# The last two QKV groups of the last head pair move one row block up in the program

## Chip, core and metric

The kernel runs on one core of a Trainium2 chip. The metric is the device time of one execution in microseconds (us). The program is written with a tile framework: a scheduler orders the instructions of every engine when the program is built, and pools hand out buffers. Each engine then runs its own list strictly in order, and so does the queue in which SyncE (SP) issues DMAs.

## What is computed

One transformer block over 2048 rows of 1024 columns, in float32: layer norm, causal attention with 16 heads of 64 columns and rotary embedding, output projection, layer norm and residual, and then a feed-forward part whose weights are stored as 4-bit codes with scales. Cut to the part that the change touches:

```python
q = (layernorm(x) @ Wq).reshape(b, s, 16, 64)        # k, v likewise
q, k = rotary(q), rotary(k)
logits = where(causal, q @ k.T, -1e9) / sqrt(64)
out = softmax(logits) @ v                            # per head
x = x + layernorm(out.reshape(b, s, 1024) @ Wo)      # then the feed-forward part
```

## The kernel before

Heads are worked on in eight pairs, m = 0 to 7. The 2048 rows are cut into four blocks of 512, J or c = 0 to 3.

**QKV groups.** `qkv(m, c, ...)` computes q, k and v of the pair m for the row block c. Each of the three is a sum of 24 matmuls with 512 columns (`mm3`, L112 to L114, each product in three parts), so a group has 72. The sum for q or k is copied out by ScalarE (ACT, L251), rotated on VectorE (DVE, L253 and L254) and GpSimd (POOL, L255 and L256), split into a high and a low part (ACT L120, DVE L121) and written to DRAM by L259, to `qs` or `ks`. v is copied (L241), transposed (PE, L244), split and written to `vs` by L249. The group first loads four tiles of the normalized input (`xc<-xd`, L222) and the rotation table (`tab`, L232).

**Attention.** `attend(h, J, ...)` handles one head and one block of 512 query rows. `scores` does two matmuls for each block of keys (L278, L280), a row maximum on DVE (L284 or L286), the exponential on ACT (L288), small DVE steps that combine the maxima and sums (L297 to L305, with one ACT step, L300), and the scaling of the probabilities on POOL (L310). `weighted` transposes the probabilities (PE, L320), splits them (ACT L120, DVE L121) and multiplies by v (L324, L325). The result of a head goes out by ACT L327 and DVE L328 and is written to `at` by L329. Keys, values and queries are loaded from DRAM by L335, L336 and L342.

**The last pair.** The loop over pairs 0 to 6 computes the groups of later pairs beside the attention. The groups (7, 2) and (7, 3) are left out of it and stand in the last loop, over J, for the pair m = 7. Before that loop the weight tile of the last part of the output projection is prepared (`last_wo`); after it come the other seven (`prep_wo`: load `wof` by L427, ACT L429, POOL L430), and then the projection of the first four row tiles (`attended`: load `af` by L456; `project`: L469 to L471), written to lie beside the last attention. All of these draw on the same four buffers of the tag `f4`: the table, the split results of q, k and v, the `wof` tiles and the `af` tiles.

**What sets the order.** The scheduler takes instructions by a priority that follows program order, as soon as its own model finds their inputs ready. A piece of the program that stands earlier is served first; one that stands later fills gaps. So the place of `group` in the loop does not fix when it runs, only who goes first where both could.

Of the kernel before, what the change touches and what calls it, by code (L numbers as in the profile page):

```python
# [57 lines left out]
def block_kernel(ctx, tc, x, wq, wk, wv, wo, gu_codes, gu_scales, d_codes, d_scales, cos_sin, out):  # L58
# [159 lines left out]
    def load_x(c):  # L218
        tiles = []
        for kp in range(4):  # L220
            tiles.append(slot("xc", [P, 2, 2, 512], FR, "xc"))
            load(f32(tiles[kp]), xd[c][:, kp])  # L222
        return tiles

    def prep_qkv(m, tags=("w", "w", "w")):
        behind = (None, high[-1], high[-1]) if m == 0 else (None,) * 3
        return [prep_w(w, m, sc, tag, b) for w, sc, tag, b in zip((wq, wk, wv), (0.125, 1.0, 1.0), tags, behind)]

    def qkv(m, c, ws, xs, ramp=False, pace=None):
        cs = slice(c * 512, (c + 1) * 512)  # L230
        tab = slot("f4", [P, 2, 512], F32, "tab")
        (A.dma_start if ramp else load)(tab, cos_sin[:, :, cs])  # L232
        for n, w in enumerate(ws):
            o = bank("S" if ramp and n != 1 else "F", "qkv")
            for k in range(KE):
                mm = mm3(o, w[k], xs[k // 2][:, :, k % 2, :], k == 0, k == KE - 1)
                if k == 0 and pace:
                    pace(mm, n)
            t1 = slot("t2", [P, 512], F32, "t1")
            if n == 2:  # L240
                A.copy(t1, o)  # L241
                pv = bank("F", "pv").rearrange("p (t n) -> p t n", t=4)
                for t in range(4):
                    T.transpose(pv[:, t, :], t1[:, t * P : (t + 1) * P], ident)  # L244
                vo = slot("f4", [P, 4, 2, 2, D], FR, "vo")
                src = pv.rearrange("p t (a d) -> p t a d", a=2)
                for a in range(2):
                    split(vo[:, :, a, 0, :], vo[:, :, a, 1, :], src[:, :, a, :])
                load(vs[m][cs].rearrange("(t p) a n -> p t (a n)", p=P), f32(vo.rearrange("p t a l d -> p t (a l d)")))  # L249
            else:  # L250
                A.copy(t1, o)  # L251
                sh = slot("t2", [P, 512], F32, "sh")
                V.stream_shuffle(sh, t1, [i ^ 1 for i in range(32)])  # L253
                V.tensor_tensor(t1, t1, tab[:, 0, :], ALU.mult)  # L254
                G.tensor_tensor(sh, sh, tab[:, 1, :], ALU.mult)  # L255
                G.tensor_tensor(t1, t1, sh, ALU.add)  # L256
                hl = slot("f4", [P, 2, 512], FR, "hl")
                split(hl[:, 0, :], hl[:, 1, :], t1)
                load((qs, ks)[n][m][:, :, cs], f32(hl))  # L259
# [71 lines left out]
    def load_kv(h, k, v, cs):  # L331

        m, r = h // 2, h % 2 * D
        for a in range(2):
            load(f32(k[a * D : (a + 1) * D, cs]), ks[m][r : r + D, a, cs])  # L335
        load(f32(v[:, cs.start // P : cs.stop // P]), vs[m][cs, h % 2, :].rearrange("(t p) n -> p t n", p=P))  # L336

    def load_q(h, q, J):

        m, r = h // 2, h % 2 * D  # L340
        for a in range(2):
            load(f32(q[a * D : (a + 1) * D]), qs[m][r : r + D, :, J * 512 : J * 512 + 512])  # L342
# [24 lines left out]
    def new_kv():  # L367
        return slot("hd", [P, S], FR, "k"), slot("hd", [P, NT, P], FR, "v")

    def new_q():  # L370

        q = slot("hd", [P, 2, 2, 512], FR, "q")
        return [q[:, 0], q[:, 1]]

    def attend(h, J, q, k, v, anchors):
        weighted(h, J, scores(J, q, k, anchors), v)
# [7 lines left out]
    def group(m, c, xs=None, pace=None):  # L384
        if m not in ws:
            ws[m] = prep_qkv(m)
        qkv(m, c, ws[m], xs or load_x(c), pace=pace)
# [47 lines left out]
    m = KE - 1  # L435
    kv = {}
    for J in range(NC):
        for h in (2 * m, 2 * m + 1):
            if J == 0:
                kv[h] = new_kv()  # L440
            load_kv(h, *kv[h], parts[J])
            if h % 2 == 0:
                qj = new_q()
            load_q(h, qj[h % 2], J)
        for h in (2 * m, 2 * m + 1):
            attend(h, J, qj[h % 2], *kv[h], anchors)
        if J in (1, 2):
            group(m, J + 1)


    wot = [prep_wo(k, "w" if k < 3 else "xc") for k in range(KE - 1)] + [last_wo]
# [388 lines left out]
```

## Time and profile before

| | |
|---|---|
| runs shown | 3012.16, 3017.91 and 3018.1 us, median 3017.91 us |
| profiled execution | 3014.01 us, of which the span of the trace is 3012.1 us |
| PE busy | 2917.0 us, 97% of the span, 14168 matmuls |
| DVE, ACT, POOL busy | 2035.8, 1698.4 and 953.0 us |
| mean granted TensorE clock | 0.991 |
| first and last matmul start of qkv with `xc` | 201.0 and 1339.4 us |

Times in the trace are counted from the start of the span. PE is the matmul engine, "SPq" the queue of SyncE. An entry such as "[2.77 <-DMA wof<-in_wo]" behind an instruction says that its engine sat idle for 2.77 us before it, and what ended this. A busy PE is not PE at its peak, since ends of matmuls are modelled and the clock may be lowered.

### The profile page before, as it was taken

The page shows a single profiled execution, that of the slowest core. Times are in us where ns is not written, and L with a number is a line of the kernel's source. Part 1 is how long each engine was busy: PE and PEld are TensorE (multiplying, and loading weights), DVE is VectorE, ACT ScalarE, POOL GpSimd, SP SyncE. Part 2 cuts the span into 40 slices and gives each one's busy share as a digit, 9 for nine tenths or more (in the row PEclk, how much of TensorE's full clock was granted, in tenths as well). Part 3 has the DMA queues.
Part 4 walks back from the last instruction along what each step waited for, and adds up shares of the span by engine and source line. Part 5 has one row for each costly group of instructions (what it writes and reads, how often), then busy time and mean ns, then how long its engine had stood idle before and what let it go on. Part 6 is the DMA issues. An engine that isn't in the chain of part 4 may idle for free.

```text
span 3012.1 us, 42532 instructions
## 1 busy us (share of the span) xinstructions
PE 2917.0 (97%) x14168; PEld 2409.7 (80%) x14168; DVE 2035.8 (68%) x4171; ACT 1698.4 (56%) x3569; POOL 953.0 (32%) x1055
## 2 busy tenths in 40 slices
PE   7989999999998999999999999999999999999998
PEld 6868888787887787777788788888888887888887
DVE  6567778886777778777665767776666677444347
ACT  4256667776666667667555655655555566333234
POOL 4344344443434343445322121222211223100034
PEclk9999999999999999999999999999999999999999
DMA  8787665757556468463456444444334444744446
GB/s 287 277 249 233 214 222 177 222 161 220 172 195 182 146 202 260 137 210 105 123 187 213 130 134 143 151 133 140 131 119 140 138 153 146 254 141 148 150 144 234
DMA packets 271740, 536.01 MB, mean 178 GB/s; under 512 B 22944, under 2 KB 113056, under 8 KB 255648
## 3 DMA queue, kind: packets, MB, share of 16 engines
q1 hardware_dynamic: 269344, 529.10, 54.6%
q10 hardware_dynamic: 2176, 4.19, 0.4%
q8 instruction: 112, 1.84, 0.3%
q14 instruction: 108, 0.88, 0.1%
HBM read 371.98 MB, written 161.22 MB: 177 GB/s over the span
## 4 chain that ended last, share of the span: by engine, by line
PE 79%; DMA 10%; DVE 4%; ACT 2%; POOL 2%; issue 1%; SPq 1%; POOLq 0%; ACTq 0%; DVEq 0%
PE bk L112 14%; PE bk L114 14%; PE bk L113 14%; PE pt L320 6%; PE qkv L112 4%; PE qkv L113 4%; PE qkv L114 4%; PE o L325 3%; PE o L324 3%; PE s L278 3%; PE s L280 3%; DMA wf<-in_wq 3%; PE pj L469 2%; PE pj L471 2%; PE pj L470 2%
## 5 line engine op out<-in xcount | busy, mean ns | idle before, releaser
L310 POOL TENSOR_SCALAR prob<-prob,rc 128x512 f32<-128x512 f32 (+3 forms) x640 | 405.4, 659 | 436.4 <-DVE rc L305 219.6
L112 PE MATMUL bk<-x,wt 128*128 128x512 f32 x1376 | 534.0, 390 | 2.7 <-ACT wt L120 1.8
L113 PE MATMUL bk<-x,wt 128*128 128x512 f32 x1376 | 535.2, 389 | 0.0
L114 PE MATMUL bk<-x,wt 128*128 128x512 f32 x1376 | 535.1, 389 | 0.0
L288 ACT ACTIVATE prob<-s,mxs 128x512 f32<-128x512 f32 (+3 forms) x640 | 402.6, 632 | 147.8 <-DVE mxs L286 90.6
L121 DVE TENSOR_TENSOR pw<-pt,pw 128x512 fp32r<-128x512 f32 (+3 forms) x640 | 378.4, 602 | 119.7 <-ACT pw L120 118.0
L534 ACT ACTIVATE ln<-cs,bias 128x512 f32<-128x512 f32 x520 | 360.0, 716 | 109.2 <-DVE m L541 25.4
L120 ACT CAST pw<-pt 128x512 fp32r<-128x512 f32 (+3 forms) x640 | 324.1, 527 | 171.6 <-PE pt L320 140.6
L320 PE MATMUL pt<-ident,prob 128*128 128x128 f32 x2176 | 345.5, 275 | 6.8 <-DVE pw L121 5.5
L320 PEld LDWEIGHTS pt<-ident,prob 128*128 128x128 f32 x2176 | 267.6, 141 | 61.7 <-issue 7.2
L112 PEld LDWEIGHTS bk<-x,wt 128*128 128x128 f32 x1376 | 258.2, 188 | 57.5 <-ACT wt L120 2.6
L286 DVE TENSOR_REDUCE mxs<-s 128x1 f32<-128x512 f32 x384 | 260.9, 681 | 60.0 <-PE s L280 59.1
L114 PEld LDWEIGHTS bk<-x,wt 128*128 128x128 f32 x1376 | 258.3, 188 | 53.8
L113 PEld LDWEIGHTS bk<-x,wt 128*128 128x128 f32 x1376 | 258.3, 188 | 53.5
L278 PE MATMUL s<-k,q 128*128 128x512 f32 (+3 forms) x640 | 265.7, 416 | 25.1 <-ACT prob L288 22.4
L325 PE MATMUL o<-pw,v 128*128 128x512 f32 (+3 forms) x640 | 247.3, 388 | 9.5 <-DVE pw L121 9.0
L324 PE MATMUL o<-pw,v 128*128 128x512 f32 (+3 forms) x640 | 244.3, 382 | 9.8 <-ACT pw L120 7.9
L112 PE MATMUL qkv<-xc,w 128*128 128x512 f32 x576 | 231.8, 402 | 10.3 <-ACT w L186 6.3
L113 PE MATMUL bk<-bt,at 128*128 128x512 f32 x616 | 239.6, 389 | 0.0
L114 PE MATMUL bk<-bt,at 128*128 128x512 f32 x616 | 238.8, 389 | 0.0
L112 PE MATMUL bk<-bt,at 128*128 128x512 f32 x616 | 238.7, 389 | 0.0
L280 PE MATMUL s<-k,q 128*128 128x512 f32 (+3 forms) x640 | 236.6, 372 | 0.0
(150 smaller groups left out, 5513.8 us busy)
## 6 DMA issues: line engine op xcount, KB each, us to landing
xc<-xd SPq DMA_DIRECT2D x96, 1024.0 KB, 9.3
q<-qs SPq DMA_DIRECT2D x128, 256.0 KB, 7.2
ast<-S SPq DMA_DIRECT2D x44, 512.0 KB, 3.9
cs<-in_gu_scales SPq DMA_DIRECT2D x172, 128.0 KB, 3.2
cs<-in_gu_codes SPq DMA_DIRECT2D x86, 256.0 KB, 3.0
A<-in SPq DMA_DIRECT2D x66, 256.0 KB, 2.0
S<-in SPq DMA_DIRECT2D x66, 256.0 KB, 3.2
ast<-A SPq DMA_DIRECT2D x33, 512.0 KB, 4.5
```

What stands on the lines that cost most here:

```text
L112: r = T.matmul(o, lhsT=w[:, 0], rhs=xx[:, 0], start=first, stop=False)
L113: T.matmul(o, lhsT=w[:, 0], rhs=xx[:, 1], start=False, stop=False)
L114: T.matmul(o, lhsT=w[:, 1], rhs=xx[:, 0], start=False, stop=last)
L121: return V.tensor_tensor(lo, src, f32(hi), ALU.subtract)
L278: mm = T.matmul(s, lhsT=q[:, 0, j * P : (j + 1) * P], rhs=k[:, b:e], start=True, stop=False)
L280: T.matmul(s, lhsT=q[:, 1, j * P : (j + 1) * P], rhs=k[:, b:e], start=False, stop=True)
L288: A.activation(prob[i][:, j, : e - b], s, AF.Exp, bias=mx, scale=sign, accum_out=sums[:, j % BATCH, i : i + 1])
L310: G.tensor_scalar(p, p, rc[:, jj % BATCH, i : i + 1], 0.0, ALU.mult, ALU.add)
L320: T.transpose(pt[:, j * P : (j + 1) * P], prob[kb // 4][:, j, kb % 4 * P : (kb % 4 + 1) * P], ident)
L324: T.matmul(o[:, cs], lhsT=v[:, kb, :], rhs=pw[:, 0, cs], start=kb == 0, stop=False)
L325: T.matmul(o[:, cs], lhsT=v[:, kb, :], rhs=pw[:, 1, cs], start=False, stop=kb == nk - 1)
L534: A.activation(ln, c8, AF.Prelu, bias=bias_of[ab], scale=ab[0], alpha=ab[2])
```

## The change

The group for block J + 1 was called after the attention on block J, for J = 1 and 2. Now the group for block J + 2 is called after the attention on block J, for J = 0 and 1. So the two groups (7, 2) and (7, 3) keep their work, buffers and inputs, and each stands ahead of one more call pair of `attend` than before: (7, 2) ahead of the attention on J = 1, and (7, 3) ahead of that on J = 2.

```diff
         for h in (2 * m, 2 * m + 1):
             attend(h, J, qj[h % 2], *kv[h], anchors)
-        if J in (1, 2):
-            group(m, J + 1)
+        if J in (0, 1):
+            group(m, J + 2)
```

## The prediction

> **What bounds the kernel now.** I read the page first, then the busy time in three stretches around the last head pair, then PE's waits, then the order of time there.
>
> ```profile
> PE 2917.0 (97%) x14168; PEld 2409.7 (80%) x14168; DVE 2035.8 (68%) x4171; ACT 1698.4 (56%) x3569; POOL 953.0 (32%) x1055
> ```
>
> PE is the bound nearly everywhere, so the change can only move time where PE idles or is slowed. The instruction orders of the two kernels as built show where that can be. On PE both lists hold 14170 instructions, the first 6370 and the last 6658 alike; on DVE, ACT, POOL and SP there is likewise a common head and a common tail. Laid on the trace, the differing PE rows run from 1271.7 us to about 1503 us. Everything outside is untouched, and inside no instruction is added or removed. The busy time (PE, PEld, DVE, ACT, POOL, then clock, DMA share and GB/s) in that region:
>
> ```profile
> 1264.00:1343.00 79.00, 77.25 (x426) 65.29 (x427) 57.65 (x161) 51.95 (x138) 38.50 (x49) 1.00 0.70 224
> 1343.00:1373.50 30.50, 22.26 (x118) 17.21 (x116) 25.85 (x54) 25.97 (x61) 23.51 (x21) 0.89 0.62 205
> 1373.50:1503.00 129.50, 124.27 (x635) 101.28 (x633) 83.67 (x201) 77.27 (x175) 50.27 (x63) 1.00 0.34 106
> ```
>
> PE idles 1.75 us in the first stretch, where the groups (7, 2) and (7, 3) fill it; 8.2 us in the second, between the last group and the first projection; 5.2 us in the third, spread over many waits under 1 us. The middle one matters. Its PE waits (total, times, longest):
>
> ```profile
> PE pt L320 <- DVE pw L121: 4.7, 2, 2.5
> PE o L324 <- ACT pw L120: 2.2, 1, 2.2
> PE s L278 <- ACT prob L288: 0.7, 1, 0.7
> PE o L325 <- DVE pw L121: 0.6, 1, 0.6
> ```
>
> And how the first two came about, in order of time, SP's queue first, then the engines:
>
> ```profile
> 1338.28 0.56 SPq L259 DMA_DIRECT2D ks<-hl  x1
> 1343.80 2.37 SPq L335 DMA_DIRECT2D k<-ks  x4
> 1346.21 1.53 SPq L427 DMA_DIRECT2D wof<-in_wo  x3
> 1348.51 0.55 SPq L249 DMA_DIRECT2D vs<-vo  x1
> 1355.53 0.93 SPq L336 DMA_DIRECT2D v<-vs  x2
> 1356.50 0.98 SPq L427 DMA_DIRECT2D wof<-in_wo  x2
> ```
> ```profile
> 1350.46 1.04 ACT L429 CAST wo<-wof 128x1024 fp32r<-128x1024 f32 x1 [2.77 <-DMA wof<-in_wo]
> 1351.72 0.33 PE L324 MATMUL o<-pw,v 128*128 128x128 f32 x1 [2.22 <-ACT pw L120]
> 1351.91 2.05 DVE L299 TENSOR_TENSOR cf<-mxs,nm 128x4 f32<-128x4 f32 x1
> 1355.31 1.09 PE L320 MATMUL pt<-ident,prob 128*128 128x128 f32 x4 [2.15 <-DVE pw L121]
> 1370.51 0.63 PE L320 MATMUL pt<-ident,prob 128*128 128x128 f32 x4 [2.52 <-DVE pw L121]
> ```
>
> Group (7, 3) writes its keys at 1338.28. SP reaches the load of the same keys and stands until the write has landed, at 1343.80; the first weight tile of the output projection is queued behind the four key loads and is issued at 1346.21. ACT reaches that tile's cast at 1347.69 and waits 2.77 us, the `pw` copy behind it is late, and PE loses 2.22 us. Then a DVE step of four elements takes 2.05 us (the median of L299 is 0.163 us) while POOL runs L430, and PE loses 2.15 us; a like pile-up on DVE costs 2.52 us at 1370.5. Also the clock drops:
>
> ```profile
> 1354.00:1358.00 4.00, 2.69 (x11) 2.43 (x12) 3.92 (x11) 3.95 (x10) 3.74 (x2) 0.50 0.68 221
> ```
>
> From the mean clock of the 4 us windows around it, half clock lasted from about 1352.7 to 1359.5 us. Four transposes took 1.09 us instead of 0.60. From 1355.31 to 1359.58 PE did work that takes about 2.15 us at full clock, so the slow clock cost about 2.1 us.
>
> **The change part by part.** Nothing is added. I weigh what is moved by the PE work in front of it: 0.227 us for a matmul of 512 columns (starts at 1338.08 and 1338.31), 0.113 us for a transpose, in each kernel's order.
>
> *The groups themselves.* Each still starts when the scheduler finds its input tiles. With PE work counted from one common row, k of (7, 2) ends after 25.5 us of work instead of 26.3, q and k of (7, 3) after 53.2 and 65.1 instead of 55.9 and 66.9; v of both ends at the same row in both kernels. So "one block sooner" is 1 to 3 us on the chip, not the length of a block. The matmuls are the same 144: 0 us. The cover is the attention beside them; PE's 1.75 us of idle in this stretch is the floor of what can be gained, and I take 0 here, between -1 and +1.5 us.
>
> *Who could use q, k and v sooner.* The key loads of J = 2 were issued by 1317 us and those of J = 3 by 1346 us; the first exponentials on them come at 1354 and 1407 us. So the attention on J = 2 and 3 was not waiting for the groups: gain 0.
>
> *Loads in SP's queue.* For (7, 2) the key write passes the value loads of the pair, one write of `at` and four query loads; its loads no longer stand ahead of a blocked queue. It also puts a key load ahead of `tab` of (7, 3), which was issued at 1305.74 and used at 1321.63: a delay of a few us is covered. The second half of the input tiles of (7, 3) is then free of the key write ahead of it; PE waited 0.09 us for it. Together 0.
>
> *The stall at 1350.* The keys of (7, 3) are ready 1.9 us of PE work sooner, and their split stands six DVE rows and four ACT rows further up. Their write passes four query loads and a write of `at`. So SP's stand ends about 1.9 to 2.5 us sooner, at about 1341.6; four key loads (2.4 us) and one query load that now lies between (0.6 us) follow, and the first `wof` is issued at about 1344.6 instead of 1346.2. With the 4.2 us of its transfer, ACT's wait shrinks from 2.77 to about 1.1 us: -1.6 us. The two scale loads moved behind `wof` feed a later stage and cost 0.
>
> *What is late next.* POOL's L430 and the fourth `wof`, which is issued when the first L430 ends (1353.94 and 1353.97), follow that shift. The fifth and sixth do not: they stand in SP's queue behind the value loads, which wait for `vs` to land. In the new DVE order one row maximum more (0.6 us) comes ahead of the last split of v, so `vs` is written 0 to 1.7 us later, and ACT reaches the fifth cast sooner. It had no wait before (1362.04); now 0 to 2.5 us. I take 0.8, so the gain left of this chain is 0.8 us.
>
> *The stall at 1370.* The DVE rows L305 (1.43 us there, beside POOL's L430) and one row maximum move behind the `pw` split for which PE waited, so the 2.52 us shrink by 1 to 2 us. Against it, the seventh cast and a step that needs DVE's L299 now stand ahead of a `pw` copy on ACT: 0 to 2 us. I take -0.7.
>
> *The projection.* Its first matmul stands after 90.3 instead of 92.9 us of work, so PE has 2.6 us more to lay into the gap, if `a2` is there: it hangs on the load `af`, issued at 1364.01 after the write of `at`, whose place is unchanged. Between -1 and +2 us; 0.
>
> *The tail of the region.*
>
> ```profile
> 1468.33 1.92 DVE L121 TENSOR_TENSOR a<-af,a 128x1024 fp32r<-128x1024 f32 x1 [2.72 <-ACT a L120]
> 1470.28 0.37 SPq L456 DMA_DIRECT2D af<-at  x1
> 1476.38 1.05 ACT L120 CAST a<-af 128x1024 fp32r<-128x1024 f32 x1 [0.96 <-DMA af<-at]
> ```
>
> The load of a later row tile is issued when DVE has freed its buffer, and took 6.1 us. In the new ACT order only three instructions (an exponential, a row scaling and a `pw` copy) lie between the two casts instead of seven. The copy waits for transposes that stand behind 22 projection matmuls, so ACT comes there some 7 us after the first cast starts; the load needs 7 to 9 us. PE lost 1.7 us here; it may lose 0 to 3.5: taken as 0, the range is -1.5 to +2.
>
> *The clock.* If the first PE gap shrinks, PE may stay busy enough to keep full clock: -2.1 or 0. It fell here after two gaps of 2.2 us close together, with PE busy 1.44 of 4 us. One gap of two will probably stay; I take 0.
>
> The Trainium skill ("TensorE: Matmul & The Clock Gate", Part 1: The HAM clock gate) says that the array drops to half rate after at least one idle window of about 3.4 us. No gap here is longer than 2.52 us, and yet half clock came, so the row decides; by the page there was nothing to lose and nothing to regain here, by the row 2.1 us.
>
> **The sum.** -0.8 - 0.7 = -1.5 us, against the profiled execution's 3014.01 us: 3012.5 us. That execution lies 3.9 us under the median of the runs shown; the mean of all four is 3015.5 us, and I place the forecast on it: 3014.0 us. About 0.2%, or 6 us, is what a measurement of this kernel can tell from no change, so this is no change.
>
> **The rivals.** First, *the stretch without filler closes* (faster). The gaps of 2.2, 2.15 and 2.5 us hang on one chain from the late `wof`; with that in time, most of them and the half clock go: 6.9 + 2.1 = 9 us at most, some 7.5 us with a remainder: 3008 us. For it: the load is issued sooner, and the projection stands nearer. Against it: L299 beside L430 and the fifth `wof` do not move.
>
> Second, *the cast of a weight tile waits longer in ACT's queue* (slower). The place is the fifth to seventh L429, behind loads that SP issues after the value loads. If `vs` lands late, ACT stands up to 5.5 us (the median landing of `wof`), `pw` and the exponentials behind it wait too, PE idles as long, and another half-clock period is added (2.1 us): +7 us, 3022.5 us. It decides from an ACT wait of some 5 us on, beyond the 1.6 us that the first cast gains. For it: PE has no QKV work left there. Against it: these loads were issued 3.8 to 6.4 us ahead of need.
>
> Third, *the change does not do what it says*: the scheduler put the groups where they were already. The row counts above show this nearly so; it gives 0, 3015.5 us, and lies in the forecast's case.
>
> **How the numbers follow.** The forecast with the third rival 0.45; faster 0.27; slower 0.28. The attention lists are interleaved anew over 1142 PE rows, and small in-order waits that I can't price could add up on either side, hence the weight of the last two. The forecast's own range is 3009 to 3020 (-5 to +4 us on the mean). The whole range takes in both rivals, short of their ends: 3006 to 3025 us.
>
> **What would show it.** Right: ACT's wait at the first L429 of the middle stretch is 0.5 to 1.5 us; the PE gap there is under 1 us; the sum of PE's idle from 1264 to 1503 us is within 4 us of 15.2; nothing outside differs. Wrong: a PE gap over 4 us at any `pw`, an ACT wait over 3 us for `wof` or `af`, or a second half-clock period; and for the faster case, no half clock between 1340 and 1380 us.

## The result, and the profile after

The changed kernel is slower by about 6 us. Its median is 3021.42 us (13 runs, 3019.15 to 3028.9), that of the kernel before, measured beside it, 3015.38 us (13 runs, 3010.21 to 3020.33); the ratio is 1.0021 with a 95% interval of 1.0012 to 1.0029. The forecast, no change, was wrong: the measured median lies above its own range (3009 to 3020 us), and inside the whole range (3006 to 3025 us).

The page shows PE a little busier, with the same 14168 matmuls:

```profile
PE 2920.4 (97%) x14168; PEld 2411.0 (80%) x14168; DVE 2037.9 (68%) x4171; ACT 1697.2 (56%) x3569; POOL 948.1 (31%) x1055
```

**Where the time went.** Both lists hold the same work between two common PE rows, 6340 and 8000. From the start of one to the start of the other the changed kernel takes 8.1 us longer in its profile; in a second profile of it 6.35 us longer, and a second profile of the kernel before differs from the first by 0.7 us. The profiled executions (3020.90 and 3014.01 us) differ by 6.9 us, so nothing outside this region adds to the loss. The same three stretches as in the prediction, for the changed kernel (busy time of PE, PEld, DVE, ACT, POOL, then clock, DMA share and GB/s):

```profile
1264.00:1343.00 79.00, 77.98 (x430) 65.48 (x429) 61.77 (x161) 52.46 (x139) 34.73 (x46) 1.00 0.69 210
1343.00:1373.50 30.50, 19.66 (x95) 15.71 (x94) 20.93 (x46) 22.94 (x53) 21.19 (x15) 0.78 0.69 214
1373.50:1503.00 129.50, 124.51 (x615) 99.72 (x614) 87.68 (x206) 77.85 (x178) 50.79 (x68) 0.97 0.35 107
```

PE's idle time hardly grew: 16.9 us over the three rows, against 15.2 before. What grew is hidden in the column of the clock: 0.78 in the middle stretch against 0.89, and 0.97 in the third against 1.00. A slow PE counts as busy, so a table of busy time alone shows no loss. The half-clock periods in the traces last 3.41 us or a multiple of it. These are the first such step in question, at full clock, and then all steps of this region at half clock:

```profile
1347.41:1350.82 3.41, 1.34 (x10) 1.06 (x8) 0.68 (x3) 0.45 (x1) 0.00 (x0) 1.00 1.03 380
1350.82:1364.48 13.66, 9.40 (x32) 7.55 (x33) 8.45 (x15) 10.64 (x23) 11.95 (x8) 0.50 0.80 261
1374.72:1378.14 3.42, 3.42 (x10) 2.70 (x9) 3.11 (x6) 1.15 (x3) 3.17 (x4) 0.50 0.51 96
1490.77:1494.19 3.42, 3.42 (x10) 2.68 (x9) 1.69 (x6) 0.94 (x3) 3.42 (x7) 0.50 0.98 329
```

At half clock, matmuls of 512 columns start 0.43 us apart (1361.38, 1361.81 and 1362.23) instead of 0.23, so PE does about half the work in its busy time. As an estimate, these rows cost (9.40 + 3.42 + 3.42) / 2 = 8.1 us. The account from 1262 to 1525 us, for two profiles of each kernel (idle time in gaps over 0.15 us):

| us | before | before, again | after | after, again |
|---|---|---|---|---|
| PE idle | 14.9 | 15.3 | 17.3 | 15.7 |
| lost to half clock | 2.3 | 2.6 | 8.1 | 6.4 |
| sum | 17.2 | 17.9 | 25.4 | 22.1 |

Between the first profiles 5.8 us of the loss are clock and 2.4 us idle time, between the second ones 3.8 and 0.4 us; the latter is 4.2 of the 5.7 us by which the region differs there. By the PE work done (means of two profiles each), the loss lies in three places: +1.3 us while the groups still run, +4.7 us in the 20 us of PE work behind them, +2.2 us in the tail around 1490 us. Between the last two it is -0.4 us, and at the very start, where the lists are still alike, -0.8 us, which is chance.

**The middle stretch.** PE's waits there (total, times, longest):

```profile
PE s L278 <- ACT prob L288: 3.4, 1, 3.4
PE pt L320 <- DVE pw L121: 2.9, 2, 2.3
PE pt L320 <- DVE sm L304: 2.5, 1, 2.5
PE s L278 <- DVE ol L328: 1.5, 1, 1.5
```

And SP's queue, then the engines, in order of time:

```profile
1335.75 0.54 SPq L259 DMA_DIRECT2D ks<-hl  x1
1336.62 1.88 SPq L342 DMA_DIRECT2D q<-qs  x3
1338.59 0.55 SPq L329 DMA_DIRECT2D at<-ol  x1
1339.24 2.48 SPq L335 DMA_DIRECT2D k<-ks  x4
1341.76 0.60 SPq L342 DMA_DIRECT2D q<-qs  x1
1342.80 1.92 SPq L427 DMA_DIRECT2D wof<-in_wo  x3
```
```profile
1344.27 0.58 ACT L327 COPY ol<-o 64x512 f32<-64x512 f32 x1 [0.84 <-DMA at<-ol]
1345.60 0.50 PE L278 MATMUL s<-k,q 128*128 128x512 f32 x1 [1.48 <-DVE ol L328]
1350.37 1.04 ACT L429 CAST wo<-wof 128x1024 fp32r<-128x1024 f32 x1 [3.63 <-DMA wof<-in_wo]
1352.15 0.47 PE L278 MATMUL s<-k,q 128*128 128x128 f32 x1 [3.40 <-ACT prob L288]
1354.43 4.66 POOL L430 TENSOR_TENSOR wo<-wof,wo 128x1024 fp32r<-128x1024 f32 x2 [0.57 <-ACT wo L429]
1359.86 0.87 PE L320 MATMUL pt<-ident,prob 128*128 128x128 f32 x3 [2.31 <-DVE pw L121]
```

The key write stands further up and the first `wof` is issued at 1342.80, 3.4 us sooner than before. It lands no sooner in the order of the work: 7.6 us after its issue instead of 4.2 us (6.7 and 4.8 us in the second profiles), behind eight loads of q and k that were issued in the 6.2 us ahead of it. So ACT's wait did not shrink. The gap of PE behind it is now 3.40 us. That leaves PE 1.34 us of work in one clock step, and the next four steps go at half clock: in the first three of them PE was again busy for only 2.09, 2.69 and 1.21 us. Another gap, of 1.48 us, comes just before, in a step in which PE was busy 1.93 us and the clock held.

No matmul of the groups is left at this place in either kernel. The last one starts at 1340.1 us before (1339.4 in the table of the kernel before is the start of its weight load) and at 1339.1 us after, behind 72.6 and 72.8 us of PE work counted from row 6340.

### The profile page after: what moved, and what is told of

It reads as the page before. It is cut to its first block, busy times and chain, and to the rows that moved or that the text cites. A ratio compares the mean times of both kernels' runs of the same rounds, so it can differ in the third digit from the quotient of the medians.

```text
span 3019.1 us, 42529 instructions
## 1 busy us (share of the span) xinstructions
PE 2920.4 (97%) x14168; PEld 2411.0 (80%) x14168; DVE 2037.9 (68%) x4171; ACT 1697.2 (56%) x3569; POOL 948.1 (31%) x1055
## 4 chain that ended last, share of the span: by engine, by line
PE 78%; DMA 11%; DVE 4%; ACT 3%; issue 1%; POOL 1%; SPq 1%; POOLq 0%; ACTq 0%; DVEq 0%
PE bk L112 14%; PE bk L113 14%; PE bk L114 14%; PE pt L320 6%; PE qkv L112 4%; PE qkv L113 4%; PE qkv L114 4%; PE o L325 3%; PE o L324 3%; PE s L278 3%; PE s L280 3%; DMA wf<-in_wq 3%; PE pj L469 2%; PE pj L471 2%; PE pj L470 2%; DMA xc<-xd 2%
## 5 line engine op out<-in xcount | busy, mean ns | idle before, releaser
L324 PE MATMUL o<-pw,v 128*128 128x512 f32 (+3 forms) x640 | 244.9, 383 | 6.1 <-ACT pw L120 4.2
```

The costliest lines, as they stand in the source:

```text
L324: T.matmul(o[:, cs], lhsT=v[:, kb, :], rhs=pw[:, 0, cs], start=kb == 0, stop=False)
```

## Experiments

"After" in an edit means the changed kernel. `after(x, y)` places the instruction x behind y in the scheduler's order. Every ratio is to the kernel before, measured on the same chip beside the run, with its 95% interval. The diffs show the lines that carry each edit, not every helper line. A line number of a kernel with added lines is moved by them: L440 or L433 is the cast L429, L434 the step L430, and in the rows with L440 and L331 the matmul L327 is L324 and DVE's L331 is L328.

**How large is the difference?** The changed kernel again, and the kernel before again, with no edit.

> The changed kernel once more, for a second profile. Theory A: again an ACT wait of over 3 us at the first weight cast, a PE gap of over 3 us behind it, over 10 us of half clock between 1340 and 1380 us: 3020 to 3023 us. Theory C: again 32 to 34 us from PE row 7380 to 7512. Theory D (the half-clock periods fall by chance, the rest of the lists is as good as before): the clock periods lie elsewhere and the cost of the middle stretch is 2 us or less this time.

> The kernel before once more, for a second profile of it. If the account by traces holds, ACT again waits 2 to 3 us at the first weight cast, the half clock between 1262 and 1525 us is 3.4 to 10.2 us (2 to 5 us of lost time), less than the 10 to 20 us of the profiles of the changed kernel; ratio 0.999 to 1.001.

Measured: 3020.39 us, 1.0018 [1.0009, 1.0027], for the changed kernel, and 3016.99 us, 1.0004 [0.9993, 1.0016], for the kernel before. The loss is real, 5 to 6 us, and one ratio is good to 1 in 1000. The profile of the kernel before shows the wait of ACT for the first `wof` at 3.54 us and a PE gap of 2.99 us behind it:

```profile
1351.75 1.04 ACT L429 CAST wo<-wof 128x1024 fp32r<-128x1024 f32 x1 [3.54 <-DMA wof<-in_wo]
1353.01 0.33 PE L324 MATMUL o<-pw,v 128*128 128x128 f32 x1 [2.99 <-ACT pw L120]
```

So the length of that wait is not what sets the kernels apart: it is 2.77 and 3.54 us in the one, 3.63 and 2.92 us in the other. Nor is the PE gap behind it, 2.22 and 2.99 us against 3.40 and 2.69 us. Two more runs below, on the tail, have the changed kernel's lists in the middle stretch. In all four profiles of these lists there is the gap for `ol` (1.48 to 1.86 us), which the kernel before does not have, and 4.7 to 7.0 us lost to half clock between 1340 and 1380 us, against 2.3 and 2.6 us.

**Which of the two groups?** Only (7, 2) moved up:

```diff
-        if J in (0, 1):
-            group(m, J + 2)
+        if J == 0:
+            group(m, 2)
+        if J == 2:
+            group(m, 3)
```

> Group (7, 2) stands one block sooner as in the change, group (7, 3) stays where it was before. From PE row 6936 of 14170 on the list is that of the kernel before; the first weight tile of the projection is again behind the four key loads of a later key write. Theory A (in the changed kernel the first weight tile lands late among the q and k loads, ACT stands at its cast, PE idles 3.4 us and the clock falls to half for longer): ACT's wait at the first weight cast 2 to 3 us, half clock in 1340 to 1380 us about 7 us, time 3014 to 3017 us. Theory B (the loss comes with group (7, 2) itself, through the attention lists before row 6611, which are those of the changed kernel): 3020 to 3023 us. Theory C (the loss comes in the tail, where the cast of an input tile of the projection stands sooner in ACT's queue): the tail is that of before, so 3 us come back and 3 stay: 3017 to 3019 us.

Measured: 3018.17 us, 1.0013 [1.0003, 1.0023]. (7, 2) alone gives about two thirds of the loss, within a wide interval. The other half was not run: with (7, 3) alone moved up, every engine's instruction list is that of the kernel before. Then both groups right behind the first block:

```diff
-        if J in (0, 1):
-            group(m, J + 2)
+        if J == 0:
+            group(m, 2)
+            group(m, 3)
```

> The dose: both groups directly after the first block, one block sooner still for (7, 3). Theory A: the key loads again stand ahead of the weight tiles, ACT waits 2.5 to 4 us at the first cast: 3019 to 3024 us. Theory B (sooner is dearer): 3022 to 3028 us. If the loss came from the particular interleaving of the changed kernel alone: 3013 to 3017 us.

Measured: 3025.06 us, 1.0033 [1.0019, 1.0047], the slowest of all. As a measure of how early the groups run I take the PE work on attention that stands ahead of one of their 144 matmuls, on the mean, from a common row: 21.9 us before, 21.4 with (7, 2) alone, 20.8 after, 20.0 here. The ratios go the same way: 1, 1.0013, 1.0018 to 1.0021, 1.0033. The ends of this row are clear of each other, its neighbours are not. It is four program orders and no more than a trend: by another measure, the PE work ahead of the groups' last matmul, they are 72.6, 73.8, 72.8 and 70.3 us, which does not follow the ratios. In the last kernel a gap of 6.46 us took part, which the section on the hardware shows.

**The first weight tile.** The key loads of J = 3 are put behind the first three `wof` loads, in the changed kernel and in the kernel before; for that, these loads, with their casts and low parts, also move up in the program, ahead of the attention on J = 3:

```diff
-            load(f32(k[a * D : (a + 1) * D, cs]), ks[m][r : r + D, a, cs])
+            ld = load(f32(k[a * D : (a + 1) * D, cs]), ks[m][r : r + D, a, cs])
+            if behind:
+                after(ld, behind)
...
+        if J == NC - 1:
+            wot = [prep_wo(k, "w") for k in range(3)]
...
-            load_kv(h, *kv[h], parts[J])
+            load_kv(h, *kv[h], parts[J], wof[2] if J == NC - 1 else None)
```

> The changed kernel with the key loads of J = 3 put behind the first three weight tiles of the projection in SP's queue. Theory A: the first weight tile is issued some 3 us sooner and lands in 4 to 6 us, ACT's wait at its cast falls from 3.63 to under 1 us, PE's 3.4 us gap goes, half clock is there for 7 us or less: 3012 to 3016 us. Theory B: the lists up to row 6817 are those of the changed kernel, so 3020 to 3023 us. Theory C: the tail from row 6930 on is that of before, so 3 us of the 6 come back: 3017 to 3019 us.

> The kernel before with the key loads of J = 3 put behind the first three weight tiles in SP's queue. Theory A: the wait of 2.77 us at the first weight cast falls to under 1 us and the PE gap of 2.2 us goes; the tail is planned anew and may give 2 us either way: 3011 to 3015 us. Theory B (the loss of the change comes with group (7, 2), not with the loads): the same for this kernel, with the changed kernel so altered 6 us above it, while the changed kernel so altered measured the same as before.

Measured: changed kernel 3017.04 us, 1.0000 [0.9989, 1.0011]; kernel before 3011.65 us, 0.9989 [0.9978, 0.9999]. ACT's first wait falls to 1.80 us in the one and to nothing in the other. This takes about 2.0 in 1000 from the changed kernel and 1.1 in 1000 from the kernel before: a stall that both share. Whether it costs the changed kernel more, these intervals do not tell. Even without keys ahead of it the first tile took 7.3 us to land in the changed kernel, behind four q loads. Next, the first two `wof` tiles go into free buffers of another tag, with their loads far ahead:

```diff
-        wf = slot("f4", [P, E], F32, "wof")
-        load(wf, wo[k * P : (k + 1) * P, :])
+        wf = slot("pb" if k < 2 else "f4", [P, E], F32, "wof")
+        ld = load(wf, wo[k * P : (k + 1) * P, :])
+        if k < 2:
+            after(ld, latest_q[0])
```

> The changed kernel with the first two weight tiles of the projection loaded into two free buffers, behind the query loads of J = 2 in SP's queue, some 20 us ahead of their casts. Theory A: ACT waits under 0.3 us for either tile, the PE gap of 3.4 us and most of the half clock go: 3009 to 3014 us. Theory B: 3019 to 3022 us, as ACT's wait was not what cost the time. Theory C: from row 7098 on the tail is that of before: 3017 to 3019 us.

> The same two free buffers in the kernel before, the groups where they were. Theory A: ACT's wait of 2.77 us and the PE gaps of 2.2 us behind it go, with them some of the half clock: 3009 to 3013 us, within 3 us of the changed kernel with the same buffers. Theory B: 3010 to 3013 us, but 6 us or more below the changed kernel with the same buffers. Theory C: the tail is that of the changed kernel, so about 3 us are lost there and 2 to 4 gained in the middle: 3014 to 3017 us.

Measured: changed kernel 3024.26 us, 1.0023 [1.0013, 1.0033], a miss; kernel before 3014.32 us, 0.9991 [0.9979, 1.0003]. The trace of the first says why: the loads came sooner, and so did the casts, and ACT waited at the first and at the third tile.

```profile
1330.76 1.05 ACT L433 CAST wo<-wof 128x1024 fp32r<-128x1024 f32 x1 [3.25 <-DMA wof<-in_wo]
1357.88 1.04 ACT L433 CAST wo<-wof 128x1024 fp32r<-128x1024 f32 x1 [3.18 <-DMA wof<-in_wo]
1360.15 0.79 PE L278 MATMUL s<-k,q 128*128 128x512 f32 x1 [3.37 <-ACT prob L288]
```

At the first wait PE stood for 0.97 us; matmuls of the groups lay beside it. The second, as long, stopped PE for 3.37 us: about the same wait of ACT with cover and without. In the kernel before with the same edit, a still longer wait fell among the groups' matmuls, and PE was busy for all of the 6 us from 1325 to 1331 us:

```profile
1329.54 1.05 ACT L433 CAST wo<-wof 128x1024 fp32r<-128x1024 f32 x1 [3.89 <-DMA wof<-in_wo]
```

Both edits together, so that three tiles are ahead of the keys:

```diff
+        wf = slot("pb" if k < 2 else "f4", [P, E], F32, "wof")
...
+            load_kv(h, *kv[h], parts[J], wof[2] if J == NC - 1 else None)
```

> The changed kernel with the first two weight tiles loaded ahead into free buffers and, new against the earlier run, the third one ahead of the key loads of J = 3. There the wait of 3.18 us had moved to the third tile. Theory A: ACT waits under 1 us at each of the first three casts, no PE gap over 2.5 us, half clock in 1340 to 1390 us 7 us or less: 3012 to 3017 us. Theory B: 3020 to 3024 us. Theory C: the tail list ends as in the changed kernel (alike from PE row 7509), so 3017 to 3020 us.

Measured: 3021.97 us, 1.0021 [1.0011, 1.0031], a second miss. The casts moved up again, with waits of 4.08 us at 1328.8 and 4.25 us at 1355 us. PE stood 1.81 us at the first and 4.30 us at the second, the same contrast again. So the casts had to be held at their old places in ACT's list, with the loads ahead (`hold[0]` is the last cast of a split in a group, `exps` the list of all exponentials):

```diff
-        A.copy(t[:, 0], wf)
+        cast = A.copy(t[:, 0], wf)
+        if k < 3:
+            after(cast, (hold[0], exps[-24], exps[-23])[k])
```

> The changed kernel with two weight tiles loaded ahead into free buffers, the third load ahead of the key loads of J = 3, and each of these casts held at the place in ACT's queue that the changed kernel gives the first, the second and about the fourth cast. PE's list is that of the changed kernel up to row 6817, ACT's up to row 1652: the first cast stands where it stood, only its data are there. Theory A: ACT's wait there is 0 instead of 2.9 to 3.7 us, the PE gap on the exponential behind it falls from 1.9 to 3.4 us to under 0.7 us, half clock in 1340 to 1376 us is 7 us or less: the stretch up to PE row 6899 costs 3 us less than in the changed kernel, 3015 to 3018 us in all. Theory B (the groups' place as such): 3020 to 3023 us with the gap gone. Theory E (the planner's list is behind the next queue, DVE beside POOL, anyway): the gap goes, another of the same size opens at a copy that waits for DVE, 3019 to 3022 us.

> The same in the kernel before: lists alike up to PE row 6817. Theory A: the wait of 2.77 us and the gap of 2.2 us go, 3010 to 3014 us, and the pair of kernels without the wait lies 4 us or less apart. Theory B: the pair lies 6 us apart, as with the wait. Theory E: 3014 to 3017 us.

Measured: changed kernel 3016.41 us, 1.0006 [0.9996, 1.0016]; kernel before 3013.48 us, 1.0002 [0.9993, 1.0011]. PE's list is the changed kernel's up to row 6817, behind the first gaps. Without the first wait the two kernels differ by 0.4 in 1000, some 1 us (2.9 us by the medians), where they differed by 2.0; the edit gains some 4 us in the changed kernel and nothing in the kernel before. The intervals of these differences are about 1.4 in 1000 either way, so the gain in the changed kernel is shown, if only just (a second run with this edit, below, agrees: 1.0007), and its size only roughly. The pair is not clean, though. In the changed kernel the first cast now waits for nothing, but the stall is not all gone, and ACT waits again at a later tile:

```profile
1347.13 1.07 ACT L440 CAST wo<-wof 128x1024 fp32r<-128x1024 f32 x1
1353.62 1.04 ACT L440 CAST wo<-wof 128x1024 fp32r<-128x1024 f32 x1 [1.99 <-DMA wof<-in_wo]
1356.04 0.80 PE L327 MATMUL o<-pw,v 128*128 128x512 f32 x1 [2.91 <-DVE ol L331]
1363.80 1.04 ACT L440 CAST wo<-wof 128x1024 fp32r<-128x1024 f32 x1 [3.62 <-DMA wof<-in_wo]
1365.57 0.79 PE L280 MATMUL s<-k,q 128*128 128x512 f32 x1 [2.94 <-ACT prob L290]
```

In the kernel before no cast waits any more, but a new gap opens, longer than the 2.22 us that went:

```profile
1356.60 0.80 PE L327 MATMUL o<-pw,v 128*128 128x512 f32 x1 [4.16 <-DVE ol L331]
```

So "nothing gained" there does not say that the wait cost nothing there.

**DVE beside POOL.** The low parts of the seven weight tiles are made by DVE instead of POOL (L430), first alone, on the kernel before:

```diff
-        G.tensor_tensor(t[:, 1], wf, f32(t[:, 0]), ALU.subtract)
+        (G if k == KE - 1 else V).tensor_tensor(t[:, 1], wf, f32(t[:, 0]), ALU.subtract)
```

> The kernel before with the low parts of the first seven weight tiles computed on DVE instead of POOL (seven instructions of 1.2 us there, by the row of the like split of an input tile, instead of 2.35 us on POOL). Lists differ by PE rows 6800 to 7098 alone. Theory E (DVE's small steps are stretched to 2 us by POOL working on the same tiles, and that is what PE's gaps of 2.15 and 2.52 us come from): no DVE step of four elements over 0.4 us between 1345 and 1376 us, both gaps under 1 us: 3012 to 3015 us. Against it (DVE has no room for 8.4 us more): gaps of 1 us or more at every pw copy, 3017 to 3021 us.

Measured: 3015.0 us, 0.9999 [0.999, 1.0009], no gain: ACT still waits for the first tile, and half clock still cost 5.9 us in this profile, with a second wait of ACT for `wof`, of 2.90 us, behind the first of 2.65. Together with the key loads behind the `wof` loads (diff above), run twice:

> The kernel before with both: key loads of J = 3 behind the first three weight tiles, and the low parts on DVE. Lists differ from those of before by PE rows 6800 to 7098 alone, so the tail is that of before. Theories A and E together: neither the wait of 2.77 us nor stretched DVE steps, half clock at most 3.4 us: 3008 to 3012 us, the fastest of all. Theory A alone: 3011 to 3014 us, as with the key loads alone.

> The fastest so far once more (kernel before, key loads of J = 3 behind three weight tiles, low parts on DVE), to narrow its interval: 3009 to 3013 us, ratio to before 0.998 to 0.9995; no half clock between 1340 and 1376 us.

Measured: 3011.37 us, 0.9988 [0.9977, 1.0], and 3009.22 us, 0.9980 [0.997, 0.9991]. This is the fastest version, and it beats both kernels; by the ratios it can't be told from the key loads alone (0.9989). The middle stretch now has 7.1 us idle and no half clock:

```profile
1343.00:1373.50 30.50, 23.40 (x119) 17.27 (x120) 27.86 (x65) 25.29 (x59) 8.50 (x12) 1.00 0.68 217
```

The same two edits on the changed kernel:

> The changed kernel with the key loads of J = 3 behind three weight tiles and the low parts of the weight tiles on DVE, which made the kernel before faster by 0.1 to 0.2%. If the wait, the stretched DVE steps and the half clock behind them are what the groups' earlier place costs, little is left of the difference: 3009 to 3014 us, within 3 us of the kernel before with the same two edits. If the earlier place costs by itself: 3015 to 3020 us.

Measured: 3022.24 us, 1.0018 [1.0007, 1.003], a miss. It lies 3 to 4 in 1000 above the same edits on the kernel before. Its trace has new waits of ACT for `af` and `wof` (1.6 to 2.8 us, five of them) and 6.1 us lost to half clock. So these two edits do not mend the new order, and its cost is not that of the first weight tile and of the stretched DVE steps alone: of the four pairs of kernels with the same edit, only one lies less than 1 in 1000 apart. What more it would take stays open.

**The tail.** First the suspicion of the prediction, the cast of a later `af` tile, put behind the exponentials in question:

```diff
+        if t == 8:
+            after(high[0], exps[-9])
```

> The changed kernel, with the cast of the input tile for t = 8 held in ACT's queue behind the last exponential of the second row block, six places further down, as before. All lists differ from those of the changed kernel by PE rows 7384 to 7526 and ACT rows 1782 to 1801 alone. Theory A (the loss lies in the middle, at the first weight casts and the half clock they bring): 3020 to 3022 us, within 1 us of the changed kernel. Theory C (the tail costs 3 of the 6 us): ACT's wait of 1.61 us for that tile and the PE gaps of 1.1 and 1.8 us go, no half clock near PE row 7429, and from row 7380 to 7512 it takes 29.9 us as before instead of 33.1 us: 3017 to 3019 us.

Measured: 3018.4 us, 1.0012 [1.0001, 1.0022]. The trace keeps the loss of half clock (8.7 us) and splits the gap in two (0.9 and 0.68 us); against the repeat of the changed kernel in the same comparison (1.0018) nothing can be told apart. What in fact stood ahead of the late exponential in the changed kernel is a normalization (L151) and a copy out:

```profile
1486.33 1.25 ACT L151 ACTIVATE y<-x,nb,rs 128x1024 f32<-128x1024 f32 x1
1487.61 0.58 ACT L327 COPY ol<-o 64x512 f32<-64x512 f32 x1
1488.21 0.69 ACT L288 ACTIVATE prob<-s,mxs 128x512 f32<-128x512 f32 x1
...
1489.04 0.50 PE L278 MATMUL s<-k,q 128*128 128x512 f32 x1 [1.81 <-ACT prob L288]
```

So that normalization was put behind the last exponential:

```diff
-        normalize(y, xt, ln_stats(halves(xt)))
+        last = normalize(y, xt, ln_stats(halves(xt)))
+        if t == 3:
+            after(last, exps[-1])
```

> The changed kernel with one normalization of a row tile (L151, 1.25 us on ACT) held behind the four exponentials that follow it in ACT's queue. In the profiles of the changed kernel it and a copy stand ahead of the exponential that frees a bank of scores, and PE waits 1.81 us there, with a half-clock period behind. Lists differ from the changed kernel by PE rows 7444 to 7586 and ACT rows 1798 to 1813 alone; PE's list up to the gap is the same. Theory F (this queue place is what the tail costs): the gap of 1.81 us falls to under 0.7 us, no half clock near it, the tail costs 1.5 to 3 us less: 3017 to 3019 us. Against it (the tail's loss moves on, as with the cast of the input tile): 3020 to 3022 us.

Measured: 3018.74 us, 1.0018 [1.0008, 1.0028]. The gap falls from 1.81 to 0.69 us and the half clock behind it is gone, but the time is not better by what the ratio can tell (2 us at most). Both mends together, the held casts and this:

> The changed kernel with both: the first weight casts at their places with their data there, and the normalization behind the exponentials. If the wait at the first weight cast and the tail are the two causes of the loss, this is within 0.1% of the kernel before: 3013 to 3017 us. If the groups' place costs by itself (theory B), 3018 us or more.

Measured, with both diffs, on the changed kernel: 3016.84 us, 1.0007 [0.9997, 1.0018], the same as without the second. The tail's 2 us are read from the traces and are not confirmed by a ratio.

## Why the prediction was wrong

The part of the kernel was right (nothing outside the region differs), and so were the links of the chain: first `wof`, cast in ACT's queue, exponentials, PE, clock. The step that failed is the clock term, "One gap of two will probably stay; I take 0". In its place the runs showed 8.1 us lost to half clock against 2.3 us, +5.8 us, between the first profiles, and 6.4 against 2.6 us, +3.8 us, between the second, where the region grew by 8.1 and 5.7 us. The term rests on a wrong reading. The prediction says that the clock fell "after two gaps of 2.2 us close together". By the trace of the kernel before, half clock began at 1352.70, and the second gap ran from 1353.16 to 1355.31. The first gap was enough; the second held the clock down for one step more:

```profile
1349.29:1352.70 3.41, 1.19 (x8) 0.84 (x8) 1.00 (x2) 2.24 (x5) 1.11 (x1) 1.00 0.96 323
1352.70:1356.12 3.42, 1.27 (x9) 1.11 (x7) 3.42 (x7) 3.42 (x8) 3.42 (x2) 0.50 0.86 280
```

So any one gap that leaves a clock step too little work has a price of its own, and the sum had none for it. A second term failed ahead of it: the first gap was to shrink to under 1 us, and it did not. Why the new order leaves such gaps is known only in part. Point by point:

- *The groups themselves, 0, -1 to +1.5.* The stretch in which they run cost +1.3 us by work done, inside the range. Their matmuls do cover waits of ACT: 0.97 against 3.37 us and 1.81 against 4.30 us of PE, in two kernels with moved casts. That the change takes such cover from the middle stretch is not shown: the groups end behind 72.6 and 72.8 us of PE work, ahead of the stall in both kernels.
- *Users of q, k and v, loads in SP's queue, 0.* Nothing contradicts them, except that the loads were priced by their issue alone; the next point shows what became of `wof`.
- *The stall at 1350, -1.6 us.* The key write passed the query loads as said, and `wof` was issued even sooner than the predicted 1344.6, at 1342.80. "With the 4.2 us of its transfer" failed: the load took 7.6 us from issue to landing, 6.7 us in the second profile. In the 4 us ahead of its issue the DMA share was 0.31 before (1342 to 1346 us) and 0.86 after (1339 to 1343), and 1.08 and 0.99 in the stretches behind it. That this crowding is the reason is not shown: with the keys behind `wof` the share ahead was 0.96 in the changed kernel and 1.01 in the kernel before, and the tile took 7.3 and 5.3 us. ACT waited 3.63 us instead of 1.1.
- *What is late next, the fifth and sixth `wof`, +0.8.* No wait of ACT there in the changed kernel, 0.
- *The stall at 1370, -0.7.* It stayed: 2.51 us (2.48 in the second profile), now behind L304 instead of the split of `pw`, against 2.52 (2.28).
- *A wait that had no term:* ACT L327 waits 0.84 us for the write of `at` that empties its only buffer, and PE 1.48 us for the `ol` behind it. In the second profile they are 0.96 and 1.61 us; the kernel before has no such pair. In the run with the later tail cast they are 1.22 and 1.86 us, and there this gap by itself brought half clock: PE busy 1.56 us of the step from 1338.21, half clock from 1341.63.
- *The projection, 0.* It began at 1373.4 instead of 1373.5 us on the clock of the trace, but with fewer attention rows done. It filled none of the gaps.
- *The tail, 0, -1.5 to +2.* At +2.2 us the size is just above the upper end of the range, but the place was another: the casts of `af` waited 1.41 and 1.61 us, and the PE gap behind the second, 1.13 us (0.38 in the second profile), is about that of the kernel before, 0.88 and 0.79 us; L151 ahead of an exponential cost 1.81 us and a half-clock step.
- *The clock, 0.* The term with the largest error, as said above. The sum of idle time, named as a sign for the forecast ("within 4 us of 15.2"), was met with 16.9 and could not see the loss. Two of the signs named against it did come: a wait of ACT for `wof` over 3 us (3.63) and more half-clock periods (1374.72 and 1490.77).

Of the rivals, the second came nearest in size (3022.5 us against 3021.42), but it put the wait at the fifth to seventh tile, and its price on a wait of 5 us. The wait was at the first tile, no longer than it could be before, so the near number is luck. The third, that the change does not do what it says, is right for the group (7, 3) by itself and wrong for the pair.

What stays open: the 1.3 us ahead of the middle and the 2.2 us of the tail are too small for a ratio good to 1 in 1000. Which of the new order's stalls make the 4.7 us of the middle is not settled: holding the first cast regained some 4 us, the two edits of the fastest version nothing. No run gave `ol` a second buffer, which would test the wait that only the new order has. Why the two edits do not help the changed kernel was read from one trace only.

## What to carry to other kernels

A wait of an engine with an in-order list costs PE little while independent matmuls lie beside it, and nearly its whole length where none do: price a stall by what runs beside it. Count PE's work per step of the clock as well as its idle time, since a stretch that drops to half clock looks busy, and one gap can be enough. And when a DMA is issued sooner, do not carry its transfer time over: its landing can stay where it was.

## What the runs showed of the hardware

**The clock.** Over the traces of this region (1300 to 1515 us, steps of 3.41 us that follow a step at full clock), PE busy for less than 1.5 us of one step was followed by half clock in 28 of 28 cases, 1.5 to 1.8 us in 9 of 13, 1.8 to 2.0 us in 3 of 17, and 2.0 us or more in none of over 1100. From a step at half clock the full clock came back in all 38 cases with PE busy for 2.99 us or more, in 2 of 4 with 2.8 to 2.99 us, and in none of 16 with less. (The steps are laid out from each trace's half-clock periods, and ends of matmuls are modelled.) The Trainium skill ("TensorE: Matmul & The Clock Gate", Part 1: The HAM clock gate) gives the same step, about 3.4 us, but has the half rate come after an idle window; here it came with PE busy for up to 1.98 us of the step.

**DVE behind POOL.** Between 1340 and 1380 us of the two profiles of each kernel, 20 of the small DVE steps with two inputs (L299, L302 and L305) took over 0.3 us, and each ended 0.02 us after an end of POOL's L430. Before: L299 took 2.05 us and ended at 1353.96, with L430 at 1353.94. After, L305 on four elements, against L430 from 1354.43 for 4.66 us (end 1359.09):

```profile
1357.24 1.87 DVE L305 TENSOR_TENSOR rc<-cf,sm 128x4 f32<-128x4 f32 x1
```

The longest is in the kernel with both groups behind the first block, where three POOL instructions in a row, with ends at 1367.28, 1369.58 and 1371.88, went by before DVE's six elements did:

```profile
1364.90 6.97 POOL L430 TENSOR_TENSOR wo<-wof,wo 128x1024 fp32r<-128x1024 f32 x3
1366.03 5.86 DVE L299 TENSOR_TENSOR cf<-mxs,nm 128x6 f32<-128x6 f32 x1
1372.55 0.80 PE L325 MATMUL o<-pw,v 128*128 128x512 f32 x1 [6.46 <-DVE pw L121]
```

The Trainium skill ("SBUF — State Buffer", SBUF: two separate sides) says that GpSimd and a DVE step with two inputs in SBUF share a pair of ports, and that the first to start holds it for its whole instruction while the other blocks. The rows agree, and add that DVE can miss its turn between POOL's instructions. On DVE itself the same 128x1024 step takes 1.21 us instead of 2.4, and in the four traces with it none of these small steps took over 0.3 us between 1340 and 1380 us:

```profile
1344.80 1.07 ACT L433 CAST wo<-wof 128x1024 fp32r<-128x1024 f32 x1
1346.60 1.21 DVE L434 TENSOR_TENSOR wo<-wof,wo 128x1024 fp32r<-128x1024 f32 x1
```
